# Two more blocks of deformable gathers move from the convolution stage into the attention stage

## The chip, the core and the metric

The kernel runs on one core of a Trainium2 chip. The time is that of one execution on the device, in microseconds (us). A core has TensorE for matrix products (PE in the profile; PEld is its weight load), VectorE (DVE), ScalarE (ACT), GpSimd (POOL) and SyncE (SP), which here only issues transfers. Each engine works off its own list of instructions in order and waits on semaphores for the others. Transfers between the device's memory and the core's memory run on 16 DMA engines; a gather by index is issued by POOL, plain transfers mostly by SP.

## The reference

Four layers on an input of 2 images, 256 channels, 64 x 64 pixels, all in float32:

```python
x = attention_block(x)        # group norm, qkv, 4 heads over 4096 pixels, projection, + normalized x
x = x + position_term         # a linear map of 4 coordinates
x = bottleneck(x)             # 1x1 conv to 64, deformable 3x3 with a mask, 1x1 conv to 256, + x
h = relu(group_norm(x))       # last layer: two deformable 3x3 convolutions on 256 channels
h = deform_conv(h, ...1)
h = relu(group_norm(h))
x = x + deform_conv(h, ...2)
```

A deformable 3x3 convolution works out two offsets for each pixel and each of the 9 taps, here from a 7x7 depthwise and a 1x1 convolution that are merged into one. At each shifted place it interpolates between four neighbouring pixels and multiplies what it gets by the 3x3 weights:

```python
sampled = v00 * (wy0 * wx0) + v01 * (wy0 * wx1) + v10 * (wy1 * wx0) + v11 * (wy1 * wx1)
out = einsum('bckhw,ock->bohw', sampled, w)
```

## The kernel before, in words

**Two stages.** `attention` runs first and `deform` after it. The bottleneck (`class Bottleneck`) has no stage of its own: its steps are generators that the other two call a bit at a time.

**Attention** goes through 1024 tiles `n`, two in each turn of its loop. Four units of 256 tiles are the two images times the two pairs of heads; 16 tiles are one block of 256 query pixels. For each tile PE makes scores (L580), DVE takes their maximum (L592), ACT the exponential (L598), PE transposes it (L610), DVE and ACT copy it (L627, L629), and PE multiplies it by the values (L639). At the end of a block the shares of its four key ranges are combined: `spread` transposes them (L502), DVE copies them out (L504), SP stores them to `share_d` (L506) and loads them spread over the partitions as `f` (L510), and POOL multiplies and adds in `combine` (L519, L520, L525, and L527 in units 0 and 2). DVE copies the next block's products into the same buffer `o` (L471), which has one copy. A dictionary `own` holds which step belongs to which tile. Where a tile has no step of its own, `small` calls `background` in units 2 and 3, and each turn calls it once more. `background(count)` takes `count` steps of the generators in `back`.

**What runs in the background.** In unit 2 `first_batch` starts: the bottleneck's convolution of image 0 (`conv(0)`, 144 steps of two gathers each, L848 into `bfour`; DVE weighs in L1067, POOL adds in L1077 and L1078; four steps of gathers are ahead) and then `early_image`, which normalizes the result and writes it in pixel order to `img3`. In unit 3 `early_samples` follows. It works out offsets and weights of the first blocks of deform (`EARLY` = 2 blocks of 512 pixels; `offsets` L805, L825, L839 on PE, `corners` on DVE). Then `sample` is called in each turn, once, or twice at three turns in eight: it gathers 128 pixels for one tap (512 KB, L848) into a spare buffer of attention and stores them in order to `samp_d` (L1261, on SP). The spare buffers are `xb`, and from the end of the offsets `v`, `k` and `bx` as well, eight in all.

**Deform** goes through 1152 steps `s`: four layers (two images times two convolutions) of 8 blocks of 36 steps (9 taps times 4 groups of 128 pixels). A step's four neighbours come by a gather from `img3` (L848 into `four`); in the first two blocks they come from `samp_d` by a plain load on SP (L1448; the first eight are issued on POOL). Interpolation has two ways:

- *By axis* (a paired step): ACT scales 512 columns (L1471), DVE adds the other 512 (L1477), then ACT 256 (L1486) and DVE 256 (L1490).
- *By corner* (`w4`, four products): ACT 256 (L1486) and DVE three times 256 (L1496).

PE transposes the sample (L1508), ACT copies four of them (L1517), and PE multiplies by the weights (L1527). Beside the steps run `Side` generators with a rate each: `seconds` is the bottleneck's convolution of image 1 (`conv(1)`, 288 gathers, all of its adding on DVE), `offs` the offsets of later blocks, `images` the normalization of the next image (L1372, L1382, L1388).

**What sets the order.** `run` hands the framework the order of PE, ACT, DVE and POOL as written. SP is not in that list: its order comes from the framework's own planning.

Of the kernel before, what the change touches and what calls it, by code (L numbers as in the profile page):

```python
# [11 lines left out]
F32 = mybir.dt.float32  # L12
BF16 = mybir.dt.bfloat16
I32 = mybir.dt.int32
# [6 lines left out]
P = 128  # L21
B, C, H, W = 2, 256, 64, 64
HW = H * W
NB = HW // 512
CM = 64
K2 = 9
EPS = 1e-5
DWK = 7

EARLY = 2  # L30


GH, GW = H + 1, W + 2
# [31 lines left out]
class Net:  # L65
# [115 lines left out]
    def attention(self, bott):  # L181
# [5 lines left out]
        with ExitStack() as ctx:  # L187
# [489 lines left out]
            while n < last + 4 or back or more or any(own.values()):  # L677
                u, d = divmod(n, per_unit)
                if d == 0 and u < len(units):
                    plan_unit(u)  # L680
                    if u == 0:
                        back.append(prepare(1))
                    if u == 1:
                        back.append(bott.before(0, bt, ps))
                    if u == 2:
                        back.append(first_batch())
                    if u == 3:
                        back.insert(0, bott.before(1, bt, ps))
                        back.append(self.early_samples(bott, bt, held, xp, vp, kp, ps))

                def small(at):
                    steps = own.pop(at, ())
                    for f in steps:
                        f()
                    if not steps and u > 1:
                        background(1)

                if n - 1 in pts:
                    p = pts.pop(n - 1)
                    keep(n - 1, p, "ACT")  # L700
# [24 lines left out]

                for _ in range(1 + (n % 16 in (10, 12, 14))):
                    more = self.sample()
                n += 2


    def corners(self, i, pt, mask, base, idx, w4, pool, w=None):
# [13 lines left out]
            nc.scalar.activation(mk, mk, AF.Exp, scale=-1.0)  # L745

        nc.vector.tensor_scalar(p, p, float(H), -1.0, ALU.min, ALU.max)
        whole = pool.tile([P, 4, K2, 2], I32, name="whole")
        nc.vector.tensor_copy(whole, p)
        yield True  # L750
        f = pool.tile([P, 4, K2, 2], F32, name="floor")
        nc.vector.tensor_copy(f, whole)
        g = pool.tile([P, 4, K2, 2], F32, name="above")
        nc.vector.tensor_tensor(g, f, p, ALU.is_gt)
        yield False
        nc.vector.tensor_tensor(f, f, g, ALU.subtract)
# [13 lines left out]
        if mask:  # L770
# [3 lines left out]
            for s in range(2):  # L774
                nc.vector.tensor_mul(w[:, s, :, :, 1], w[:, s, :, :, 1], mk)
            yield False
        for s in range(4):
            nc.vector.tensor_mul(w4[:, :, :, s], w[:, s % 2, :, :, 0], w[:, s // 2, :, :, 1])
        yield True

# [75 lines left out]
    class Bottleneck:  # L856
# [3 lines left out]

        GROUPS = [(0, 1), (2, 3), (4, 5), (6, 7), (8,)]

        CORNERS = NB + EARLY + 1

        def __init__(self, ctx, net):
            self.net = net
# [31 lines left out]
            self.od = wp.tile([P, 512], F32, name="bod")  # L898
            nc.gpsimd.memset(self.od, 0.0)

        def pools(self, ctx, gathers=5, sums=8):
            self.ahead = gathers - 1
            tc = self.net.tc
            return self.kept | {
                n: ctx.enter_context(tc.tile_pool(name=f"bt_{n}", bufs=bufs))
                for n, bufs in (("g", gathers), ("s", sums), ("t", 6), ("x", 2))
            }
# [306 lines left out]
                        nc.sync.dma_start(dst, t[64 * r : 64 * r + 64])  # L1214
                yield True

    def early_samples(self, bott, pools, held, xp, vp, kp, ps):


        nc, a = self.nc, self.a  # L1220
# [26 lines left out]
        for cb in range(2):  # L1247
            t = pools["x"].tile([P, 2, 512], F32, name="bx").rearrange("p u n -> p (u n)")
            whole.append(t)
            wf.append(t[:, : T * 2 * K2].rearrange("p (t o) -> p t o", o=2 * K2))  # L1250
            self.filters(wf[cb], cb, dw, pw)
            yield True
        free = deque(x.rearrange("p u n -> p (u n)") for x in xbs)
        gathers, stores = deque(), deque()

        def gather():


            if len(stores) > 1 and len(free) < 3 or not gathers and stores:
                dst, four = stores.popleft()  # L1260
                nc.sync.dma_start(dst, four)  # L1261
                free.append(four)
            if gathers:
                dst, idx = gathers.popleft()
                four = free.popleft()
                self.gather(four, self.img3[0], idx)
                stores.append((dst, four))
            return gathers or stores

        self.sample = gather  # L1270
        for i in range(EARLY):
            idx = bott.corner.tile([P, 4, K2], I32, name="bidx")
            w4 = self.early[i] = bott.corner.tile([P, 4, K2, 4], F32, name="bw4")
            steps = self.offsets(
                i, xs,
                lambda s, row: wf[s][:, DWK * row : DWK * row + DWK, :].rearrange(
                    "p t o -> p (t o)"
                ),
                self.vec[:, V_PWB : V_PWB + 1],
                bott.base, idx, w4, pools["work"], wide, ps,  # L1280
                odp=lambda: pools["t"].tile([P, 512], F32, name="bst"), y0=rows(i)[0],
                later=ps.later,
            )
            mine = False
            for done in steps:
# [15 lines left out]
    def deform(self, bott):  # L1301
# [5 lines left out]
        with ExitStack() as ctx:  # L1307
# [90 lines left out]
                        yield  # L1398

            IMAGE = 4 + 6 * NB + 1  # L1400
            corners = {(0, 0, i): (None, w4, None) for i, w4 in self.early.items()}

            def offsets(b, l):
                if b == 0:
# [1 line left out]
                wf = self.wf  # L1406
                for i in range(EARLY if (b, l) == (0, 0) else 0, NB):
                    idx = cp.tile([P, 4, K2], I32, name="didx")
                    w4 = cp.tile([P, 4, K2, 4], F32, name="dw4")
                    w = cp.tile([P, 2, 4, K2, 2], F32, name="dwt")  # L1410
                    corners[b, l, i] = idx, w4, w
                    yield from self.offsets(
# [44 lines left out]

            def paired(s):
                n, i, _, j = parts(s)
                return s < ALL and (i >= EARLY if n == 0 else j % 2 == 1)  # L1460

            def share(s, side, axis):
                n, i, k, j = parts(s)
# [77 lines left out]
            def finish(n, i, ob, s):  # L1541
# [14 lines left out]
                        lambda: nc.vector.bn_stats(stats[b][:, ob, i, :], xs)  # L1556
                    )
                else:
                    res = work.tile([P, 512], F32, name="res")
                    nc.sync.dma_start(res, self.x2d[b][rows, cols])  # L1560

                    def second_layer():
# [18 lines left out]
                            self.steps = None  # L1581

            OFFS = 24
            inner = ExitStack()
            second = bott.conv(1, bott.pools(inner, 8, 7), ps)
            for s in range(AHEAD):
                gather(s)
# [3 lines left out]
            next(begun)  # L1591
            load(0, self.xn_d[0], wp)
            offs = [Side(EARLY * BLOCK - LEAD - 6, OFFS / BLOCK, begun)]
            first(0)


            last = Side(0, 1, bott.last(1, bott.kept, ps))
            seconds = Side(0, 0.9, second, lambda s: 2.5 * min(s, EARLY * BLOCK))
            stats[0] = self.norm_stats()
            images = []  # L1600
            for s in range(ALL + 16):
# [15 lines left out]
                if seconds:  # L1617
                    seconds.follow(s)
                    if not seconds.steps:
                        seconds = None  # L1620
                        stats[1] = bott.stats[1]
                        inner.close()
                        images.append(Side(s, 0.9, image(*layers[1])))
                if s % LAYER == LAYER // 2 and 1 <= n < len(layers) - 1:
                    images.append(
# [111 lines left out]
```

## Time and profile before

| | us |
|---|---|
| median of 3 runs (5121.92 to 5128.18) | 5122.12 |
| the profiled execution | 5119.31 |
| its span | 5117.5 |
| PE busy | 4793.9 |
| DVE busy | 4025.2 |
| ACT busy | 3251.1 |
| POOL busy | 2325.6 |

The mean granted clock of TensorE is 0.972. Attention ends near 2965 us; the first step of deform starts at 2990.6. In the page, slices are 128 us each, and a digit is the busy share in tenths. A group line gives busy time and mean of one in ns, then the idle time just before and what ended most of it. In a timeline, a start, a time, an engine, a line and its tiles.

### The profile page before, as it was taken

What the parts mean: (1) busy time and instruction counts of PE and PEld (TensorE: products, weight loads), DVE (VectorE), ACT (ScalarE), POOL (GpSimd) and SP (SyncE); (2) the same over time, 40 slices, a digit from 0 to 9 for tenths busy, and PEclk for the clock granted to TensorE, in tenths of its full rate; (3) what the DMA queues carried; (4) which work ended last, traced back from release to release, by engine and by line L of the source; (5) the groups of instructions that cost most, each with busy time, mean ns of one, the idle gap of its engine ahead of it and who ended that gap; (6) DMA issues with size and microseconds to landing.
All of it is one profiled execution on the core that took longest, in us unless ns stands there. A gap on an engine that the chain in (4) does not pass through costs nothing. (4 is left out here: it accounts for less than half of the span.)

```text
span 5117.5 us, 100364 instructions
## 1 busy us (share of the span) xinstructions
PE 4793.9 (94%) x38200; PEld 2669.1 (52%) x38200; DVE 4025.2 (79%) x7281; ACT 3251.1 (64%) x5869; POOL 2325.6 (45%) x2256
## 2 busy tenths in 40 slices
PE   8999999999999999999999956678999999999998
PEld 5555565555565555565555523334444444444444
DVE  6878867878768888677767668867788888888888
ACT  5676656666666666666656622247876766666666
POOL 0111111111106777565123257775777666666665
PEclk9999999999999999999999977779999999999999
DMA  5231121111112333332547767679999999999998
GB/s 173 61 97 53 43 69 49 35 47 31 55 53 80 103 98 105 93 86 70 164 147 284 274 223 236 202 237 349 358 339 352 363 376 358 366 396 344 349 352 331
DMA packets 367025, 997.68 MB, mean 195 GB/s; under 512 B 61372, under 2 KB 98810, under 8 KB 366542
## 3 DMA queue, kind: packets, MB, share of 16 engines
q0 software_dynamic: 196560, 690.41, 37.4%
q1 hardware_dynamic: 169438, 300.73, 18.0%
q8 instruction: 300, 4.92, 0.4%
q14 instruction: 183, 1.50, 0.1%
q10 hardware_dynamic: 544, 0.13, 0.0%
HBM read 855.36 MB, written 127.35 MB: 192 GB/s over the span
## 5 line engine op out<-in xcount | busy, mean ns | idle before, releaser
L598 ACT ACTIVATE e<-sc,low 128x1024 f32<-128x1024 f32 x1024 | 1146.2, 1119 | 742.3 <-DVE low L592 738.0
L848 POOL DMA_INDIRECT four<-img,didx x1080 | 1152.6, 1067 | 549.9 <-issue 140.3
L592 DVE TENSOR_REDUCE low<-sc 128x1 f32<-128x1024 f32 x1024 | 1205.0, 1218 | 231.7 <-PE sc L580 227.3
L1527 PE MATMUL out<-st,wc 128*128 128x512 f32 x2304 | 1224.8, 614 | 85.7 <-ACT st L1517 41.5
L580 PE MATMUL sc<-k,qs 64*128 64x512 f32 x2048 | 999.1, 606 | 0.5 <-DVE k L368 0.3
L639 PE MATMUL av<-et,v 128*64 128x256 f32 x8192 | 997.7, 386 | 0.0
L580 PE MATMUL sc<-k,q 64*128 64x512 f32 x2048 | 978.2, 605 | 0.0
L519 POOL TENSOR_TENSOR o<-o,f 128x1024 f32<-128x1024 f32 x63 | 149.5, 2373 | 1765.2 <-DMA f<-share_d 1007.7
L610 PEld LDWEIGHTS tt<-ident,e 64*128 64x128 f32 x16384 | 655.3, 139 | 512.9 <-issue 272.7
L629 ACT COPY et<-tt 128x512 f32<-128x512 f32 x1152 | 658.4, 584 | 171.8 <-PE tt L610 170.8
L610 PE MATMUL tt<-ident,e 64*128 64x64 f32 x16384 | 728.0, 227 | 36.3 <-ACT et L629 17.7
L627 DVE COPY et<-tt 128x512 f32<-128x512 f32 x896 | 612.5, 684 | 161.5 <-PE tt L610 160.9
L1496 DVE SCALAR_TENSOR_TENSOR smp<-four,dw,smp 128x256 f32<-128x256 f32 x1296 | 627.2, 484 | 140.5 <-ACT smp L1486 109.0
L639 PEld LDWEIGHTS av<-et,v 128*64 128x64 f32 x8192 | 554.0, 137 | 300.9 <-issue 48.4
L848 POOL DMA_INDIRECT bfour<-img,bidx x576 | 584.1, 1014 | 183.9 <-issue 94.8
L1508 PEld LDWEIGHTS pt<-ident,smp 128*128 128x128 f32 x2304 | 330.5, 144 | 633.9 <-issue 470.9
L1471 ACT ACTIVATE four<-four,dwt 128x512 f32<-128x512 f32 x648 | 465.0, 718 | 200.1 <-DMA four<-img,didx 196.6
L1477 DVE SCALAR_TENSOR_TENSOR four<-four,dwt 128x512 f32<-128x512 f32 x648 | 484.9, 748 | 112.6 <-ACT four L1471 110.2
L1527 PEld LDWEIGHTS out<-st,wc 128*128 128x128 f32 x2304 | 390.9, 196 | 339.3 <-issue 222.8
L580 PEld LDWEIGHTS sc<-k,qs 64*128 64x128 f32 x2048 | 346.9, 189 | 208.7 <-issue 116.8
L1508 PE MATMUL pt<-ident,smp 128*128 128x128 f32 x2304 | 448.8, 278 | 4.6 <-DVE smp L1496 3.1
L805 PE MATMUL pd<-x,wf 128*126 128x512 f32 x840 | 436.0, 601 | 0.0
(189 smaller groups left out, 4743.1 us busy)
## 6 DMA issues: line engine op xcount, KB each, us to landing
f<-share_d SPq DMA_DIRECT2D x128, 256.0 KB
four<-samp_d SPq DMA_DIRECT2D x64, 512.0 KB
xb<-xn SPq DMA_DIRECT2D x55, 512.0 KB
img<-imgt SPq DMA_DIRECT2D x96, 256.0 KB
four<-img,didx POOLq DMA_INDIRECT x1080
xa<-res SPq DMA_DIRECT2D x32, 512.0 KB
samp_d<-xb SPq DMA_DIRECT2D x32, 512.0 KB
xb<-in_x SPq DMA_DIRECT2D x20, 512.0 KB
```

The source lines that it names most:

```text
L580: nc.tensor.matmul(s[:, j, :], lhsT=q[u, i // 2][int(h != j)][halves[j], at : at + P], rhs=k[u][c][halves[j], h, :], start=True, stop=True,)
L592: nc.vector.tensor_reduce(low, s, AX.X, ALU.max, negate=True)
L598: nc.scalar.activation(e.rearrange("p j n -> p (j n)"), s, AF.Exp, bias=blk.low[:, g, c : c + 1], accum_out=blk.sum[:, g, c : c + 1],)
L610: nc.tensor.transpose(pt[:, m, :], e[half, m // 4, m % 4 * P : m % 4 * P + P], self.ident[half, half],)
L627: nc.vector.tensor_copy(dst, pt)
L629: nc.scalar.copy(dst, pt)
L639: nc.tensor.matmul(now["av"][halves[h], :], lhsT=v[u][c][:, m, halves[h]], rhs=ets[j][:, m, h, :], start=(m == 0), stop=(m == 7),)
L848: self.nc.gpsimd.indirect_dma_start(out=dst, out_offset=None, in_=img, in_offset=bass.IndirectOffsetOnAxis(ap=idx, axis=0),)
L1477: nc.vector.scalar_tensor_tensor(uv, four[:, 2 * C :], share(s, 1, 1), uv, ALU.mult, ALU.add)
L1496: nc.vector.scalar_tensor_tensor(smps[s], four[:, c], weight(s, c), smps[s], ALU.mult, ALU.add)
L1508: nc.tensor.transpose(pts[u][:, c, j * P : (j + 1) * P], smp[:, c * P : c * P + P], self.ident,)
L1527: nc.tensor.matmul(outs[ob], lhsT=wc[k][:, c, ob * P : ob * P + P], rhs=sts[u][:, c, :], start=(k == 0 and c == 0), stop=(k == K2 - 1 and ...
```

## The change

- `EARLY` is 4 instead of 2: two more blocks have their offsets worked out and their 72 gathers done during unit 3 of attention, and deform reads 144 steps from `samp_d` instead of 72.
- The early blocks keep weights by axis instead of four products; in deform all steps of the first layer are paired. `w4` is not made there.
- `small` takes two background steps instead of one where `n % 4 == 0`; `sample` is called twice at five turns in eight instead of three.
- The spare buffers become nine (a `pos` tile more), and stores start while fewer than four are free.
- In deform `seconds` has 1.1 extra calls per step over 144 steps instead of 2.5 over 72, and the first steps' `left` and `right` are done ahead of the loop.
- For memory: `above` shares the buffer of `whole`, `bsmp` has 7 buffers in attention instead of 8, `res` of the last layers comes from a pool that is opened later, and the index buffers are 12 instead of 11.

```diff
-EARLY = 2
+EARLY = 4
...
-                        back.append(self.early_samples(bott, bt, held, xp, vp, kp, ps))
+                        back.append(self.early_samples(bott, bt, held, xp, vp, kp, one, ps))
...
                     if not steps and u > 1:
-                        background(1)
+                        background(1 + (n % 4 == 0))
...
-                for _ in range(1 + (n % 16 in (10, 12, 14))):
+                for _ in range(1 + (n % 16 in (2, 6, 10, 12, 14))):
                     more = self.sample()
...
-        whole = pool.tile([P, 4, K2, 2], I32, name="whole")
+        whole = pool.tile([P, 4, K2, 2], F32, name="whole").bitcast(I32)
...
-        g = pool.tile([P, 4, K2, 2], F32, name="above")
+        g = whole.bitcast(F32)
...
-        for s in range(4):
+        for s in range(4 if w4 is not None else 0):
             nc.vector.tensor_mul(w4[:, :, :, s], w[:, s % 2, :, :, 0], w[:, s // 2, :, :, 1])
...
-        CORNERS = NB + EARLY + 1
+        CORNERS = NB + EARLY
...
-        def pools(self, ctx, gathers=5, sums=8):
+        def pools(self, ctx, gathers=5, sums=7):
...
+        xbs.append(one.tile([P, 2, 512], F32, name="pos"))
         free = deque(x.rearrange("p u n -> p (u n)") for x in xbs)
...
-            if len(stores) > 1 and len(free) < 3 or not gathers and stores:
+            if len(stores) > 1 and len(free) < 4 or not gathers and stores:
...
-            w4 = self.early[i] = bott.corner.tile([P, 4, K2, 4], F32, name="bw4")
+            w = bott.corner.tile([P, 4, K2, 4], F32, name="bw4").rearrange("p a k c -> p (a k c)")
+            w = self.early[i] = w.rearrange("p (s j k t) -> p s j k t", s=2, j=4, t=2)
...
-                bott.base, idx, w4, pools["work"], wide, ps,
+                bott.base, idx, None, pools["work"], wide, ps,
...
-            corners = {(0, 0, i): (None, w4, None) for i, w4 in self.early.items()}
+            corners = {(0, 0, i): (None, None, w) for i, w in self.early.items()}
...
-                    w4 = cp.tile([P, 4, K2, 4], F32, name="dw4")
+                    w4 = cp.tile([P, 4, K2, 4], F32, name="dw4") if b or l else None
...
-                return s < ALL and (i >= EARLY if n == 0 else j % 2 == 1)
+                return s < ALL and (n == 0 or j % 2 == 1)
...
-                    res = work.tile([P, 512], F32, name="res")
+                    res = places["res"].tile([P, 512], F32, name="res")
...
+            for s in range(3):
+                left(s)
+            for s in range(2):
+                right(s)
             first(0)
...
-            seconds = Side(0, 0.9, second, lambda s: 2.5 * min(s, EARLY * BLOCK))
+            seconds = Side(0, 0.9, second, lambda s: 1.1 * min(s, EARLY * BLOCK))
...
                         inner.close()
+                        places["res"] = ctx.enter_context(tc.tile_pool(name="df_r", bufs=2))
```

More of the change, by code (lines that the diff above doesn't have):

```diff
@@ L1215, in early_image, with early_samples @@
                 yield True
-    def early_samples(self, bott, pools, held, xp, vp, kp, ps):
+    def early_samples(self, bott, pools, held, xp, vp, kp, one, ps):
         nc, a = self.nc, self.a
@@ L1279, in early_samples @@
                 self.vec[:, V_PWB : V_PWB + 1],
-                bott.base, idx, w4, pools["work"], wide, ps,
+                bott.base, idx, None, pools["work"], wide, ps,
                 odp=lambda: pools["t"].tile([P, 512], F32, name="bst"), y0=rows(i)[0],
-                later=ps.later,
+                later=ps.later, w=w,
             )
@@ L1583, in deform @@
             OFFS = 24
-            inner = ExitStack()
+            inner, places = ExitStack(), {}
             second = bott.conv(1, bott.pools(inner, 8, 7), ps)
```

## The prediction

> **What bounds the kernel now.** I read the slices of the page first, then busy times by stretch, then groups, waits and timelines of the two stretches that the change touches.
>
> ```profile
> PE   8999999999999999999999956678999999999998
> PEclk9999999999999999999999977779999999999999
> ...
> ```
>
> Attention (slices 0 to 22) and the last 1600 us keep PE at nine tenths; slices 23 to 27 do not, and there the granted clock falls too. Busy times by stretch (PE, PEld, DVE, ACT, POOL, clock, DMA share, GB/s):
>
> ```profile
> 3000.00:3100.00 100.00, 44.70 (x137) 22.15 (x138) 79.74 (x200) 19.26 (x35) 72.05 (x71) 0.67 0.73 248
> 3200.00:3300.00 100.00, 66.92 (x200) 30.49 (x200) 90.64 (x211) 23.45 (x42) 77.40 (x74) 0.77 0.67 213
> ...
> 3600.00:3700.00 100.00, 95.42 (x348) 48.57 (x347) 77.47 (x162) 84.95 (x150) 73.15 (x63) 1.00 0.94 348
> ```
>
> This is the start of deform (call it the dip): step 0 (first L1486) starts at 2990.6 us, step 144 at 3524, so 533 us for 144 steps, against 1.5 to 1.7 us per step after that. What fills it, groups of 3040 to 3320 (busy, mean ns | idle before):
>
> ```profile
> L848 POOL DMA_INDIRECT bfour<-img,bidx x206 | 214.6, 1042 | 62.8 <-issue 34.7 <-DMA bfour<-img,bidx 7.3 <-DVE smp L1496 6.7
> ...
> L1067 DVE TENSOR_TENSOR bfour<-bfour,bw 128x512 f32<-128x512 f32 x103 | 70.7, 686 | 15.4 <-DMA bfour<-img,bidx 14.9
> ```
>
> A gather is 1.04 us plus a constant gap of 0.30, start to start 1.35 us, and in these 280 us POOL has no other gap: POOL bounds the dip, with image 1's second convolution (288 gathers). DVE waits only 15 us for it: it is the next bound, close behind.
>
> In unit 3 of attention the early gathers already cost something. Waits of 2660 to 2960, and one round of SP:
>
> ```profile
> POOL o L519 <- DMA f<-share_d: 137.4, 6, 30.8
> DVE o L471 <- POOL avs L525: 10.4, 4, 4.4
> ```
>
> ```profile
> 2861.95 0.34 SPq L1261 DMA_DIRECT2D samp_d<-bx  x1
> ...
> 2885.30 2.79 SPq L1261 DMA_DIRECT2D samp_d<-xb  x2
> 2888.19 0.65 SPq L506 DMA_DIRECT2D share_d<-shares  x1
> 2891.98 1.11 SPq L510 DMA_DIRECT2D f<-share_d  x2
> ```
>
> The shares were copied out by DVE at 2882.1; their store starts at 2888.2, because SP still stands at samp_d stores, and POOL's next multiplication waits for them:
>
> ```profile
> 2804.50 2.36 POOL L519 TENSOR_TENSOR o<-o,f 128x1024 f32<-128x1024 f32 x1 [19.00 <-DMA f<-share_d]
> 2852.95 2.35 POOL L519 TENSOR_TENSOR o<-o,f 128x1024 f32<-128x1024 f32 x1 [24.68 <-DMA f<-share_d]
> 2896.57 2.36 POOL L519 TENSOR_TENSOR o<-o,f 128x1024 f32<-128x1024 f32 x1 [19.73 <-DMA f<-share_d]
> ```
>
> Two rounds here are 92.1 us (2804.50 to 2896.57); in unit 1, with no early gathers, two rounds are 86.3 (1178.0 to 1264.4, same line). And in unit 2 POOL is nearly full:
>
> ```profile
> 1717.76 0.96 POOL L848 DMA_INDIRECT bfour<-img,bidx  x1 [0.27 <-POOL bsmp L1078]
> 1719.03 0.95 POOL L848 DMA_INDIRECT bfour<-img,bidx  x1 [0.30 <-issue]
> 1720.37 0.72 POOL L1077 TENSOR_TENSOR bfour<-bfour 128x256 f32<-128x256 f32 x1 [0.40 <-DVE bfour L1067]
> 1721.17 0.45 POOL L1078 TENSOR_TENSOR bsmp<-bfour 128x128 f32<-128x128 f32 x1
> ```
>
> One step of the convolution there (two gathers, two additions) takes POOL about 4.15 us.
>
> **The change, part by part.** The sum is made against the profiled execution, 5119.3 us (span 5117.5); the median of the runs is 2.8 us higher.
>
> *Two more blocks leave the dip (gain 80).* Now steps 0 to 143 read samp_d through SP, and the convolution is spread over them at 0.9 + 1.1 = 2 calls per step (it was 0.9 + 2.5 over 72 steps, then 0.9); its 300 or so calls end near step 160 instead of 139. By step 144 POOL issues 288 + 8 = 296 gathers: 296 x 1.347 = 399 us from 2999, so 3398 at the earliest. DVE, from start to start of neighbouring instructions: a step by axes 0.67 (L1477) + 0.40 (L1490), both from 3760 to 3970; convolution 0.69 + 0.49 + 0.22; its tail (L1123, L1130, L1129) 1.79 x 16/144 = 0.20; together 2.66 x 144 = 383, and some 10 for index arithmetic: 393 us from about 3005. With the 5.5% that it idles in 3040 to 3320 (15.5 of 280), 416: step 144 near 3422 instead of 3524, 102 less. The stall where image 1 starts to be normalized (steps 132 to 143 take 31 us, their neighbours 20) only moves behind step 144 (12 back), and the convolution's last 17 calls do too (5), and some start-up stays: I take 80. Bounds: POOL without any gap, 3398, gives 109; DVE at the 82% of the whole dip gives 479 us, so 54, less the 17: from 37 to 109. Weights by axis in the 72 early steps are in this sum: three L1496 (1.45 us) become 1.07, and ACT gets one L1471 more (0.72 us), 52 us on an engine that is busy 189 of 534 us there; without that cover they would be paid in full. Dropping dw4 saves four L778 (0.22 us each) for four blocks, under 4 us of DVE, taken as nothing while POOL and DVE are both full; 109 holds it.
>
> *Two more blocks of offsets move into attention (cost 29).* There PE is full. The two blocks of now took 11.0 and 12.3 us of PE in L805 (28 matmuls each); a whole block has 28 x 0.43 = 12, plus 1.9 of L825 and 0.5 of L839: 14.5 each. The round with the two blocks of now was 66.0 us (2603.90 to 2669.91) instead of 43, 23 for two cropped blocks. In the dip the same matmuls lay beside POOL, so nothing comes back there. 25 to 34.
>
> *144 pairs of gather and store, 13 per round instead of 11 (cost 35).* Each pair is 1 MB; in the timeline stores follow at 2.49 us (11 stores, 2861.95 to 2887.78 at the end, DMA share 1.02 in between). A round is: combination to first store 9.0 us, the stores, then 8.4 until f lands. With 13, the short rounds go from 43.6 to 48.6. The long ones (48.4) already wait for another thing, SP at the reload of res until 39.7 us after the combination; the stores would end at 39.8: 48.9. Two rounds: 97.5, against 86.6 free. From the first early gather at about tile 820 (counted below), 144 pairs are 11 rounds; the first two carry the offsets and hide it; 9.2 x 5.4 = 50. Now it is 5.6 x 2.6 = 15. Queued behind POOL's L519 are all later gathers, behind SP's stores the shares, q halves and xb loads; DVE's L471 waits for o, and L592 and the copies of the next tile stand behind it. Bounds: if the store of the shares slips in front, 15 are won; if the long rounds grow by 5 too, 55.
>
> *Denser calls in units 2 and 3 (cost 20 and 11).* Counting the free places: 15 and 18 calls in even and odd blocks of 16 tiles become 17 and 23, so 8.25 steps (two calls each) per block become 10. POOL then needs 20 x 4.15 + 4.4 + 6.8 (combinations, with L527 in one) = 94.2 us per two blocks. PE, by the starts of L592, needs 80.7 (unit 0 has 40.3 per block) plus 20 x 0.45 (two blocks of now take 89.65 with 16.5 steps, 1.6 of them idle): 89.6. POOL becomes the bound by 4.6 per pair; 144 steps are 7.2 pairs: 33, less the 14 of idle PE now: 20, from 0 (four gathers ahead absorb it) to 45 (twice the wait). Two calls in one place also use the one PSUM bank twice with no attention between them, so PE waits for a copy (0.6 to 0.7 us and its queue): some eight in the image, a dozen in the offsets, about 0.55 each: 11; 0 to 30. In return the convolution ends some 50 tiles earlier and the early blocks start at tile 812 or so, not 888; at 13 per 16 tiles the last store is issued near tile 1005 of 1024.
>
> *One pool buffer less (bsmp 7), the aliased tiles, the res pool, the preamble of left and right:* nothing; four bsmp are filled per transposition and at most three more before it, and the others have no instruction on the path. If bsmp waits once per transposition for a PE slot (2.7 us), 40 transpositions cost 0 to 30 of POOL, inside the 45.
>
> Sum: -80 + 29 + 35 + 20 + 11 = +15: 5119.3 + 15 = 5134, as a median 5137.
>
> [...] In 1600 to 2080 L1067 takes 898 ns on DVE in the mean (median 683, longest 2430), against 686 in the dip, where POOL adds nothing: 0.21 us each, and the count of 144 stays, so the sum has nothing for it. [...]
>
> **Rivals.** (1) Faster: the store of the shares does not fall behind the stores. SP's order is not written out in the kernel (only PE, ACT, DVE and POOL are), so it may come elsewhere; then rounds are 43 us, and instead of +35 there are -15: 5087. For it speaks that the store waited 1.0 us only in the first such round, against it 5.6 and 5.8 in the next short ones. It decides below 10 us of cost. (2) No difference: POOL's four steps of lead absorb the denser calls and PE does not meet the bank, -31: 5106; with the dip's gain nearer 60, 5126. Against it, POOL's runs without a gap in unit 2. (3) Slower still: the early blocks start 50 tiles later than I count; 14 pairs are left after the last tile, 2.5 us each, with nothing beside them (+35), 5172; about the same comes from DVE at 82% in the dip (+43).
>
> **How the numbers follow.** A measurement tells about 0.2%, 10 us, from no change. My sum 0.43, rival 1 0.30, rival 2 0.12, rival 3 0.15. My own case runs from 5112 to 5165 by its bounds taken half; a sixth of it lies within 0.2%. Faster: rival 1 and a third of rival 2, 0.34; same: the rest of 2 and 0.08 of mine, 0.16; slower 0.50. The range goes from rival 1 with a dip of 85 to rival 3 with 10 on top: 5080 to 5185.
>
> **What would show it.** Right: in the dip, POOL's gathers back to back to about 3400 on the old clock of the deform start, step 144 some 430 us after step 0; in unit 3, rounds of L519 near 48.6 with L471 waiting for POOL's avs in nearly all; in unit 2, two rounds near 94 with DVE's L1067 waiting for gathers; first early gather near tile 820. Wrong: short rounds still at 43, conv rounds at 90, or early gathers still running after the last L592.

## The result and the profile after

The changed kernel takes 5197.15 us in the median of 4 runs (5192.82 to 5199.73); the kernel before, beside it on the same chip, takes 5122.82 (4 runs). The ratio is 1.0141, with an interval of 1.0127 to 1.0154: 74 us slower. The profiled execution has a span of 5193.6 us, 76.1 more than before. In the new file the lines of attention keep their numbers, those of deform are higher by two (L1486 is now L1488, L1490 L1492, L1527 L1529), and the store of a sample is L1262.

The page's slices of the kernel after (130 us each) show how the picture has turned. The weak place of before, counted from slice 0 (5, 6, 6, 7 and 8 tenths in slices 23 to 27) has become a little shallower and a slice shorter (6, 7, 7, 7 in slices 24 to 27), and three slices of attention, 18, 21 and 23, have fallen to eight tenths:

```profile
PE   8999999999999999998998986777999999999998
...
PEclk9999999999999999999998997888999999999999
```

In the dip, the stretches of the kernel after (PE, PEld, DVE, ACT, POOL, clock, DMA share, GB/s), counted from a first step at 3149.0:

```profile
3160.00:3260.00 100.00, 61.97 (x198) 28.95 (x198) 83.41 (x203) 50.57 (x86) 74.72 (x69) 0.81 0.90 307
3360.00:3460.00 100.00, 76.52 (x252) 35.96 (x250) 91.26 (x191) 54.71 (x95) 79.00 (x69) 0.88 0.87 293
```

PE issues 198 to 252 matmuls in 100 us there, against 137 to 200 before. Step 144 comes 426.1 us after step 0 (before 533.4). So the part of the change in deform worked; the loss is in attention. The lengths of its stretches, from the first L592 of a unit and the first steps of deform:

| us | before | after | difference |
|---|---|---|---|
| unit 2 | 740.1 | 803.7 | +63.6 |
| unit 3 until step 0 | 800.0 | 896.0 | +96.0 |
| steps 0 to 143 | 533.4 | 426.1 | -107.3 |
| steps 144 to 287 | 233.8 | 258.1 | +24.3 |
| steps 288 to the end | 1359.7 | 1360.4 | +0.7 |

The rest of the 76.1 us, 1.2 less, lies ahead of unit 2.

To see what the 160 us in attention are made of, PE's time is split into work and idling, since PE is the engine that attention waits for. First the stretches of units 2 and 3 before, then the same after (the columns are those above):

```profile
1450.50:2190.60 740.10, 728.74 (x7906) 438.12 (x7904) 581.22 (x831) 492.39 (x919) 446.14 (x489) 1.00 0.31 90
2190.60:2990.60 800.00, 769.00 (x7895) 455.98 (x7891) 565.85 (x907) 510.56 (x950) 268.93 (x286) 0.98 0.51 172
```

```profile
1449.30:2253.00 803.70, 756.00 (x7978) 447.35 (x7976) 602.70 (x861) 499.09 (x931) 521.79 (x585) 0.97 0.32 92
...
2253.00:3149.00 896.00, 806.82 (x7923) 467.09 (x7919) 552.81 (x893) 509.67 (x946) 259.75 (x263) 0.95 0.65 231
```

Unit 2 is 27.3 us of busy PE longer and 36.3 us of idle PE (740.10 - 728.74 = 11.4 idle before, 47.7 after); unit 3 is 37.8 busy and 58.2 idle longer. In both, the granted clock has fallen by 0.03 (from 1.00 to 0.97, and from 0.98 to 0.95). PE's groups say which instructions it is. Unit 2 before and after (busy, mean ns, then idle time before them and who ended it):

```profile
L639 PE MATMUL av<-et,v 128*64 128x256 f32 x2048 | 249.7, 386 | 0.0
...
L1088 PE MATMUL pm<-ident,bsmp 128*128 128x128 f32 (+1 forms) x112 | 18.4, 286 | 1.5 <-POOL bsmp L1078 0.7 <-DVE res L550 0.3 <-DVE shares L504 0.3
```

```profile
L639 PE MATMUL av<-et,v 128*64 128x256 f32 x2048 | 257.5, 395 | 0.0
...
L1088 PE MATMUL pm<-ident,bsmp 128*128 128x128 f32 (+1 forms) x140 | 26.2, 295 | 30.5 <-POOL bsmp L1078 29.3 <-DVE shares L504 1.0
```

Unit 3 before and after:

```profile
L639 PE MATMUL av<-et,v 128*64 128x256 f32 x2096 | 257.9, 389 | 0.0
...
L610 PE MATMUL tt<-ident,e 64*128 64x64 f32 x4128 | 190.4, 228 | 15.5 <-DVE et L627 10.4 <-ACT et L629 4.1
L805 PE MATMUL pm<-v,bx 128*126 128x512 f32 (+3 forms) x56 | 23.3, 573 | 0.0
```

```profile
L639 PE MATMUL av<-et,v 128*64 128x256 f32 x2096 | 272.8, 405 | 0.0
...
L610 PE MATMUL tt<-ident,e 64*128 64x64 f32 x4128 | 194.8, 231 | 63.6 <-DVE et L627 42.0 <-ACT et L629 21.1
L805 PE MATMUL pm<-v,bx 128*126 128x512 f32 (+3 forms) x112 | 47.8, 585 | 0.0
```

Three things are to be read from these lines. In unit 2 PE's transposition of the convolution's samples (L1088) waits 29 us for POOL's sums, where it waited 1 us before. In unit 3 PE's transposition of attention's own tiles (L610) waits 48 us longer than before, for copies of DVE and ACT that are late. And in both units the same products by the values (L639, the same count) have become slower, by 7.8 and 14.9 us. Added up over the two units, L639, L580, L610 and L544, whose counts are the same, take 31 us more busy time than before. The last section shows that this is the clock.

What is late in unit 3 is the combination of shares, as the waits of the kernel after in 2640 to 3060 show:

```profile
POOL o L519 <- DMA f<-share_d: 199.2, 8, 27.0
...
DVE o L471 <- POOL avs L525: 65.6, 9, 12.2
```

L471 on DVE now stalls in each round, 7.3 us in the mean; it did so four times for 10.4 us in all. Behind it on DVE stand L592 and L627 of the next tiles, behind them PE. One round of SP, after the combination of 2694.47:

```profile
2703.50 2.36 SPq L1262 DMA_DIRECT2D samp_d<-xb  x2
...
2724.33 5.49 SPq L1262 DMA_DIRECT2D samp_d<-xb  x3
2732.08 0.32 SPq L1262 DMA_DIRECT2D samp_d<-pos  x1
2734.67 0.32 SPq L1262 DMA_DIRECT2D samp_d<-v  x1
2735.08 0.38 SPq L506 DMA_DIRECT2D share_d<-shares  x1
2739.03 1.11 SPq L510 DMA_DIRECT2D f<-share_d  x2
```

DVE had copied the shares out 10.9 us before their store was issued: SP stood at the last of 13 stores of samples, each of which waits for its gather. In the nine rounds from 2591.2 on, the store of the shares is issued 4.6 to 14.4 us after that copy; in the five full rounds of the kernel before it was 1.1 to 7.9. The rounds that follow from it, by POOL's multiplications:

```profile
2639.65 2.36 POOL L519 TENSOR_TENSOR o<-o,f 128x1024 f32<-128x1024 f32 x1 [21.86 <-DVE low L592]
2694.47 2.34 POOL L519 TENSOR_TENSOR o<-o,f 128x1024 f32<-128x1024 f32 x1 [26.61 <-DMA f<-share_d]
2743.79 2.34 POOL L519 TENSOR_TENSOR o<-o,f 128x1024 f32<-128x1024 f32 x1 [22.58 <-DMA f<-share_d]
```

These are 54.8 and 49.3 us. Over nine rounds (2591.2 to 3053.2) the mean is 51.3; before, in the same part, rounds were 43.0 to 48.4.

### The profile page after: what moved, and what is told of

It is laid out like the page before. It is cut to its first block, busy times and chain, and to the rows that moved or that the text cites. A ratio compares the mean times of both kernels' runs of the same rounds, so it can differ in the third digit from the quotient of the medians.

```text
span 5193.6 us, 100673 instructions
## 1 busy us (share of the span) xinstructions
PE 4815.3 (93%) x38200; PEld 2666.5 (51%) x38200; DVE 3995.5 (77%) x7177; ACT 3300.6 (64%) x5941; POOL 2334.2 (45%) x2256
## 3 DMA queue, kind: packets, MB, share of 16 engines
q0 software_dynamic: 196560, 690.41, 36.6%
q1 hardware_dynamic: 190750, 378.07, 21.9%
## 5 line engine op out<-in xcount | busy, mean ns | idle before, releaser
L592 DVE TENSOR_REDUCE low<-sc 128x1 f32<-128x1024 f32 x1024 | 1205.4, 1218 | 280.0 <-PE sc L580 276.5
L1529 PE MATMUL out<-st,wc 128*128 128x512 f32 x2304 | 1228.9, 616 | 83.7 <-ACT st L1519 50.6
L848 POOL DMA_INDIRECT four<-img,didx x1008 | 1068.3, 1060 | 527.2 <-ACT smp L1488 132.8
L639 PE MATMUL av<-et,v 128*64 128x256 f32 x8192 | 1020.3, 392 | 0.0
L580 PE MATMUL sc<-k,qs 64*128 64x512 f32 x2048 | 998.5, 607 | 1.2 <-ACT e L598 0.9
L580 PE MATMUL sc<-k,q 64*128 64x512 f32 x2048 | 984.0, 606 | 0.0
L610 PEld LDWEIGHTS tt<-ident,e 64*128 64x128 f32 x16384 | 652.1, 139 | 577.1 <-issue 281.8
L610 PE MATMUL tt<-ident,e 64*128 64x64 f32 x16384 | 728.0, 227 | 87.8 <-DVE et L627 47.4
L627 DVE COPY et<-tt 128x512 f32<-128x512 f32 x896 | 612.8, 684 | 147.9 <-PE tt L610 147.4
L639 PEld LDWEIGHTS av<-et,v 128*64 128x64 f32 x8192 | 562.2, 139 | 316.7 <-issue 69.6
L848 POOL DMA_INDIRECT bfour<-img,bidx x576 | 611.3, 1061 | 182.1 <-issue 87.7
L1529 PEld LDWEIGHTS out<-st,wc 128*128 128x128 f32 x2304 | 388.4, 196 | 322.0 <-issue 205.8
L1473 ACT ACTIVATE four<-four,dwt 128x512 f32<-128x512 f32 x576 | 413.4, 718 | 135.0 <-DMA four<-img,didx 131.8
L1479 DVE SCALAR_TENSOR_TENSOR four<-four,dwt 128x512 f32<-128x512 f32 x576 | 431.2, 749 | 73.9 <-ACT four L1473 71.1
L580 PEld LDWEIGHTS sc<-k,qs 64*128 64x128 f32 x2048 | 346.6, 189 | 237.4 <-issue 147.8
L805 PE MATMUL pd<-x,wf 128*126 128x512 f32 (+2 forms) x784 | 397.4, 589 | 0.0
```

What stands on the lines that cost most here:

```text
L580: nc.tensor.matmul(s[:, j, :], lhsT=q[u, i // 2][int(h != j)][halves[j], at : at + P], rhs=k[u][c][halves[j], h, :], start=True, stop=True,)
L592: nc.vector.tensor_reduce(low, s, AX.X, ALU.max, negate=True)
L610: nc.tensor.transpose(pt[:, m, :], e[half, m // 4, m % 4 * P : m % 4 * P + P], self.ident[half, half],)
L627: nc.vector.tensor_copy(dst, pt)
L639: nc.tensor.matmul(now["av"][halves[h], :], lhsT=v[u][c][:, m, halves[h]], rhs=ets[j][:, m, h, :], start=(m == 0), stop=(m == 7),)
L805: nc.tensor.matmul(pd[:m, r0 * W : r1 * W], lhsT=wt(s, t), rhs=src[:, (y + r0 - y0) * W : (y + r1 - y0) * W], start=(n == 0), stop=(n == l ...
```

## The experiments

They landed on three chips, and on two of them the kernel before is slower, so that each ratio is against the kernel before on the same chip: 5289 us beside e1 to e4, 5310 beside c_before, c_after, e5 and e6, and 5124 beside e7, e8, e9 and v1. On the chip of 5310 the change itself was run once more, and it cost less.

> The kernel before again, for its trace beside the others on one chip. Every theory: its usual time.

> The changed kernel again, for its trace and time beside the others on one chip. Every theory: 1.2 to 1.6% slower than the kernel before.

On the chip of 5310 us the kernel after took 5326.6 us, a ratio of 1.0029 (1.0015 to 1.0043). Unit 2 is 65.0 us longer (755.0 to 820.0) and unit 3 85.9 (847.3 to 933.2), about as much as on the first chip; but the dip gives back 162.4 us (605.1 to 442.7) instead of 107. Rounds before are 49.0 to 54.9 us there already, and after 50.0 to 58.2. So the expectation of 1.2 to 1.6% was missed: what the change is worth depends on the chip.

One thing sets the two slower chips apart in every run. ACT waits there for something that the trace calls "remote", which is its word for a wait whose end it can put down to no instruction and no transfer. Ahead of ACT's copies in unit 3 of the kernel before, then of the kernel after, on the chip of 5310:

```profile
ACT et L629 <- remote: 27.8, 5, 8.4
```

```profile
ACT et L629 <- remote: 42.0, 5, 10.1
```

In the six profiled executions on a chip of 5123 or 5124, those of the result among them, ACT has no such wait. Where they fall in c_after, PE, ACT and DVE stand still together, and the shares are late before SP has anything to do with them: DVE has copied them out 43.7 to 46.8 us after the combination (29.7 to 34.7 on the first chip), and their store is issued within 1.1 us of that. So the rounds are long there for another reason than on the first chip. In the first 144 steps of deform such waits of ACT come to 150.7 us in c_before and 38.5 in c_after, which goes with the larger gain there. What they are isn't known.

**The shares on another queue (e1, e2).** The store and loads of the shares are taken off SP and issued by ACT, one and two turns of the loop later; e1 does so in the kernel after, e2 in the kernel before.

```diff
-                    nc.sync.dma_start(d, t)
+                    sends.append(store)
+                    sends.append(load)
...
+                if sends:
+                    sends.popleft()()
```

> The changed kernel with the store and the two loads of the shares issued on ScalarE's queue, one turn after the transposition, instead of SP's. If the shares' place behind samp_d stores on SP sets the rounds of unit 3, rounds between L519 fall from 48 to 54 us to 43 to 46, the waits of L471 for POOL's avs (65.6 us) fall below 10, and the time falls by 50 to 75 us, to 5120 to 5147. If the 26 transfers of 512 KB per round as such set them, rounds stay above 48 and the time above 5180. Unit 2 stays at about 804 us in either case.

> The same edit in the kernel before. By the first theory the 15 us that the rounds of unit 3 cost there go: 5100 to 5115. By the second nothing changes: 5115 to 5125.

e1: 1.0057 (1.0041 to 1.0074), e2: 1.0001 (0.9988 to 1.0014). The store's wait on SP is gone in e1, yet rounds remain at 50 to 56. The waits of e1 in 2740 to 3160 (line numbers are 7 higher in this file) show why it doesn't decide:

```profile
POOL o L526 <- DMA f<-share_d: 159.6, 6, 29.3
...
ACT et L636 <- remote: 42.8, 9, 7.2
```

ACT stands nine times, 4.8 us in the mean, at the waits that the trace calls "remote". They are not the edit's doing, since the kernel before and the kernel after have them on the other slower chip. And the shares of e1 are late ahead of their store, copied out 41.2 to 43.3 us after the combination in these rounds. In c_after, on the other slower chip, they hardly wait for SP to begin with; if that holds here too, taking them off SP could win little. The expectation of e1 was missed, e2 found no difference, and neither decides anything for the first chip.

**Thirteen pairs in a round, alone (e4).**

```diff
-                for _ in range(1 + (n % 16 in (10, 12, 14))):
+                for _ in range(1 + (n % 16 in (2, 6, 10, 12, 14))):
```

> The kernel before with two more gathers and stores per block of 16 tiles alone (13 instead of 11). By the queue of SP, its 5 rounds of unit 3 get 5 us longer each and there is one fewer: 5130 to 5150. If SP's order hides two more pairs, 5115 to 5127.

0.9982 (0.9972 to 0.9991): it costs nothing on that chip. Rounds are 48.8 to 53.9, no longer than the kernel before's 49 to 55 on a chip like it, and the gathers end 16 tiles sooner. The expectation was missed; where rounds with 11 pairs are as long already, the run says nothing on a chip where they are 43.

**The stores on another queue (e5, e9).** Instead of the shares, the stores of samples are moved, from SP to POOL, which issued their gathers; e5 in the kernel after, e9 in the kernel before.

```diff
-                nc.sync.dma_start(dst, four)
+                nc.gpsimd.dma_start(dst, four)
```

> The changed kernel with the stores to samp_d on POOL's queue (as written, six calls behind their gather), so that SP has no wait for gathers ahead of the shares and no engine gets a new wait for a transfer that is still under way. If the place of the shares on SP sets the rounds of unit 3, they fall from 48 to 54 us to 43 to 46 and the time by 45 to 75 us. If the transfers as such set them, rounds stay within 2 us and so does the time within 15.

> The kernel before with its stores to samp_d on POOL's queue alone. By the place of the shares on SP its five full rounds go to 43 to 46 us: 10 to 35 us faster. If the transfers set the rounds: within 10 us.

e5 takes 5237.2 us, against 5326.6 of the kernel after on the same chip: 89 us less (45 to 75 were expected), 0.9876 (0.9847 to 0.9904) of the kernel before. The nine rounds with 13 pairs go from 50.0 to 58.2 down to 44.6 to 47.5. The same view of POOL in e5:

```profile
2649.12 2.35 POOL L519 TENSOR_TENSOR o<-o,f 128x1024 f32<-128x1024 f32 x1 [9.85 <-DMA f<-share_d]
2694.51 2.36 POOL L519 TENSOR_TENSOR o<-o,f 128x1024 f32<-128x1024 f32 x1 [6.76 <-DMA f<-share_d]
2740.73 2.36 POOL L519 TENSOR_TENSOR o<-o,f 128x1024 f32<-128x1024 f32 x1 [10.35 <-DVE low L592]
```

And unit 3 of the kernel after on that chip, then of e5:

```profile
2269.30:3202.50 933.20, 837.15 (x7923) 477.83 (x7919) 552.49 (x893) 511.49 (x947) 260.26 (x263) 0.93 0.63 222
```

```profile
2264.60:3110.60 846.00, 792.77 (x7923) 460.06 (x7919) 551.99 (x893) 511.61 (x947) 346.65 (x407) 0.98 0.69 245
```

The same gathers, the same bytes and the same number of matmuls (7923): unit 3 is 87.2 us shorter. Half of that is idle PE (96.1 to 53.2), the other half busy PE (837.2 to 792.8), as the clock rises from 0.93 to 0.98. So it is the place of the stores, on SP or on POOL, and not the number of transfers or bytes, that makes the rounds long. With the issuing engine their DMA queue changes as well, as far as the pages tell (in that of the kernel after, SP's transfers are on a `hardware_dynamic` queue, 378.07 MB, and those of POOL on a `software_dynamic` one, 690.41 MB), which no run separates. By which wait the stores on SP do it on this chip isn't shown either: the store of the shares had not waited on SP in c_after, and what e5 no longer has in unit 3 is the wait on "remote" (42.0 us in c_after, none in e5).

For a chip like the first, e8 and v1 below, which ran on the chip of 5124, are the comparison. e8 has the stores on SP, 13 pairs in a round, shares that wait 6.0 to 14.7 us for their store in the nine rounds, and rounds of 48.5 to 54.8. v1 has the stores on POOL, 16 pairs in a round, shares whose store is issued within 0.1 us of their copy in its seven full rounds, and rounds of 45.3 to 51.0. There the wait of the shares on SP and the long rounds go together.

In the kernel before, e9's edit is worth 10 us, the least that was expected: 0.9983 (0.9973 to 0.9992), with rounds of 42.5 to 46.7 instead of 43.0 to 48.4, as far fewer rounds are held up there.

No more than 0.3 to 0.4 us of issue was moved per store (a single one takes 0.32 in the rounds of the kernel after shown here), but with it the semaphore wait ahead of each store, and the time fell by 89 us in e5.

**The denser calls, alone (e3).** In the kernel before:

```diff
-                        background(1)
+                        background(1 + (n % 4 == 0))
```

> The kernel before with the denser background calls alone. If it is POOL's lack of time in unit 2 that costs, unit 2 gets 50 to 65 us longer (804 against 740), PE's L1088 waits for POOL's bsmp 25 us or more in 1550 to 2050, and the time is 5160 to 5185, since the work that leaves unit 3 gives back about 13. If instead the seven bsmp buffers of the changed kernel are the cause, unit 2 stays within 15 us of 740.

1.0117 (1.0100 to 1.0134), some 62 us, with nothing in return. Unit 2 of e3 and PE's first wait in it:

```profile
1449.80:2264.20 814.40, 761.19 (x7978) 450.01 (x7976) 605.57 (x860) 501.39 (x930) 522.80 (x585) 0.97 0.30 91
```

```profile
PE pm L1088 <- POOL bsmp L1078: 27.6, 13, 3.8
```

The kernel before with this one edit has unit 2 of the kernel after: as long (814 to 820 on such chips), with the same clock and the same wait of L1088. On the same chip e4, which leaves unit 2 as it was, takes 751.8 us for it, 62.6 less, and L1088 waits 0.7 us there. e3 keeps all eight `bsmp` buffers, so the one that the change takes away has no part in it.

**What in the denser calls costs it (e6, e7, e8).** e6 lets DVE do POOL's two additions. e7 makes POOL's first addition small and leaves out the rest of that sum. e8 keeps the number of calls, but spreads them over the turns: two in the first of a turn's two places and one in the second, in every turn, where the change has two in both places of every other turn. (The two places are the calls `small(n)` and `small(n + 1)`.)

```diff
-                engine = (nc.gpsimd, nc.vector)[b]
+                engine = nc.vector
```

```diff
-                engine.tensor_add(four[:, :, 0:2, :], four[:, :, 0:2, :], four[:, :, 2:4, :])
+                    engine.tensor_add(
+                        four[:, :, 0:2, :8], four[:, :, 0:2, :8], four[:, :, 2:4, :8]
+                    )
```

```diff
-                        background(1 + (n % 4 == 0))
+                        background(1 + (at == n))
```

> The changed kernel with the two additions per step of image 0's convolution on DVE, as image 1 has them: POOL gives up about 1.4 of its 4.15 us per step, DVE gets about 0.7. If POOL without free time makes unit 2 longer, by making PE wait for its sums, unit 2 shrinks by 30 to 60 us and so does the time. If two calls in one place (the PSUM bank, DVE) do it, unit 2 stays or grows with DVE's 0.7 us per step, 0 to 40 us.

> The changed kernel with the first of the two additions per step of image 0's convolution cut to 8 of 64 columns on POOL (the rest of that sum is left out), so that a step takes POOL about 0.5 us less of 4.15 and DVE nothing more. If POOL without free time makes unit 2 longer, unit 2 loses 30 to 55 of the 65 us that the denser calls cost it. If the denser calls cost by their place (two in one small, PE and DVE), it loses under 15.

> The changed kernel with the same number of background calls in two blocks (40), but two at every tile n and one at n + 1 instead of two and two in every other turn. If two calls one behind the other in both places of one turn cost (the bursts), unit 2 loses 20 to 50 us. If POOL's total sets it, it stays within 10.

e6 took 5392.7 us, 66 more than the kernel after on its chip, with a unit 2 of 870 instead of 820. Both expectations were missed. L1088's wait for the sums is gone, but others took its place. Its waits in 1550 to 2050 show DVE as the bound, with POOL's gathers waiting for it:

```profile
POOL bfour L848 <- DVE bsmp L1078: 184.7, 52, 8.8
```

So DVE has no more room for the denser convolution than POOL (in part it is the chip: ACT's "remote" waits in unit 2 are 29.3 us here and 8.0 in c_after). e8 took 5195.4 us in its one run, with a unit 2 of 806.0, within 2.3 of the kernel after: that both places of a turn are doubled one behind the other is not what costs. It still puts two calls into one place, in every turn, so that it says nothing on those. e7 took 5170.1 us in its one run; its unit 2:

```profile
1449.60:2228.20 778.60, 747.23 (x7978) 444.58 (x7976) 597.91 (x860) 498.81 (x930) 455.28 (x585) 0.99 0.32 95
```

25.1 us came back, less than the 30 expected: 16.3 of idle PE (the wait of L1088 went from 29.3 to 12.9) and 8.8 of busy PE, with the clock at 0.99 instead of 0.97. POOL's additions are thus a cause. With most of POOL's extra work away (446.1 busy before, 521.8 after, 455.3 here) two fifths of the 63.6 us return. Of the 38.5 that remain, 12.2 are the same wait of L1088, shorter but still there, and some 15 are work that has only moved: 28 more L1088, 40 more L1098 and 4 more L1120 lie in unit 2 than before, and unit 3 has 11.8 us less of these lines after the change.

**A version from these (v1).** The kernel after, with the stores on POOL, denser calls in unit 3 alone, and two samples in each turn to make up for the later start:

```diff
-                        background(1 + (n % 4 == 0))
+                        background(1 + (u > 2 and n % 4 == 0))
...
-                for _ in range(1 + (n % 16 in (2, 6, 10, 12, 14))):
+                for _ in range(2):
...
-                nc.sync.dma_start(dst, four)
+                nc.gpsimd.dma_start(dst, four)
```

> A version meant to beat both: the changed kernel with the stores to samp_d on POOL's queue, two samples in every turn, and the denser calls in unit 3 alone. If the place of the shares on SP and the denser calls in unit 2 are what the change pays, unit 2 takes what it takes in the kernel before, rounds of unit 3 stay below 48 with 16 pairs each, and the time is 100 to 150 us below the kernel before on that chip. If 16 pairs fill the DMA engines, rounds go above 50 and it gains under 60.

5088.9 us: 0.9929 (0.9913 to 0.9946) of the kernel before, and below the 5114.6 of e9 on the same chip, which has two early blocks. That is 35 us less than before, where 100 to 150 were expected. The profiled execution took 5104.9, the longest of the four. Unit 2 of v1 is that of before again:

```profile
1450.00:2187.70 737.70, 726.52 (x7906) 436.15 (x7904) 580.75 (x831) 492.67 (x919) 445.21 (x489) 1.00 0.30 90
```

Unit 3 takes 868.1 us (68 more than before, 28 less than after) with 16 pairs in rounds of 45.3 to 51.0, four of the seven at or above the 48 that were expected as the most, and steps 0 to 143 take 427.0. The early gathers start at tile 874 and end at 1019 of 1024. So four early blocks are worth having once they don't stand in front of the shares and unit 2 keeps the calls that it had.

## Why the prediction was right and wrong

The sign was right: my sum was +15 us on the profiled execution, and +76.1 was measured. The time itself, 5197, lies above the range, which ended at 5185. Term by term:

*The dip, -80.* Right. Step 144 was to come some 430 us after step 0, and came after 426.1. The stretch up to step 288, where the moved convolution and the stall end up, gives 107.3 - 24.3 = 83.0 back. DVE was to be what limits it: it is at 83 to 91% in the two stretches shown, and POOL is at 75 to 79 with gathers. Behind step 144, 24.3 us were given back where I counted 17; the 144 steps themselves gained a little more than I had.

*Offsets, +29.* Right: PE's L805, L825 and L839 take 24.5 + 3.9 + 2.1 = 30.5 us more in unit 3.

*The counted places.* Right: I put the first early gather near tile 820 and the last store near 1005; the first was issued at tile 828, the last gather at 1004, the last store at 1005. Rival 3, early blocks that start 50 tiles late, didn't happen.

*Pairs, +35.* The mechanism was right, its size too small. The short rounds were to be 48.6 us and are 48.0 to 49.3. What failed is the step for the long rounds: "already wait for another thing, SP at the reload of res until 39.7 us after the combination; the stores would end at 39.8: 48.9". I took the later of two waits, but they stand one behind the other. In SP's list the last store is followed by the store of the block's result (`xa`, L557), the reload of `res` waits for that store to land, and the shares' store comes behind the reload. The kernel before in its round of 2804.50, then the kernel after in its round of 2639.65:

```profile
2838.96 0.32 SPq L1261 DMA_DIRECT2D samp_d<-bx  x1
2839.37 0.39 SPq L557 DMA_DIRECT2D xa<-res  x1
2844.18 0.37 SPq L214 DMA_DIRECT2D res<-xa  x1
2844.64 0.42 SPq L506 DMA_DIRECT2D share_d<-shares  x1
```

```profile
2680.06 0.32 SPq L1262 DMA_DIRECT2D samp_d<-xb  x1
2680.47 0.42 SPq L557 DMA_DIRECT2D xa<-res  x1
2685.28 0.37 SPq L214 DMA_DIRECT2D res<-xa  x1
2685.74 0.42 SPq L506 DMA_DIRECT2D share_d<-shares  x1
```

The last store of these rounds is issued 39.6 to 40.4 us after the combination, as written, but the reload moved behind it, from 39.7 to 44.5 to 45.6, and the rounds are 53.0 to 54.8. The shares are ready when they were before and wait 12.4 to 14.4 us on SP there. Nine rounds come to 462 us, 72 more than nine free ones of 43.3, where I had 50 in all; with the 15 that before has, +57 instead of +35, which is about the bound that I had named ("if the long rounds grow by 5 too, 55"). PE's own account has +48 for it, as idle time ahead of L610. Rival 1, in which the shares slip past the stores, didn't happen by itself; v1, with the stores on POOL, shows that its place was the right one to look at.

*Denser calls, +20 and +11.* The direction was right: "POOL becomes the bound". The expected sign of it, DVE's L1067 waiting for gathers, did not come (0.2 us in that stretch). It is PE that waits for POOL's sums at L1088: 29.3 us in 13 waits, near the 33 that I had worked out. Two blocks of unit 2 were to take 94 us and take about 100. The step that failed is "less the 14 of idle PE now", a matter of a few us. PE's idle time of before has not gone away: ahead of L610 there were 8.9 us, and there are 12.3. Idle PE is 36.3 us more in unit 2, against 31 for both terms, of which a part was meant for unit 3. The second term, two calls in one place meeting the one PSUM bank, was tested by no run, since e8 keeps two calls in one place. Rival 2, in which four steps of lead absorb the calls, is refuted by e3.

*The term that was missing: the clock.* This is the largest step that failed. The sum held only waits and work, at durations of before, and put the effect of new waits on the speed of TensorE at nothing without a reason, though the prediction had seen the clock fall in the dip. PE's own instructions became slower as well: 31.3 us over L639 (+22.7), L580 (+5.5), L544 (+1.8) and L610 (+1.3), and 4.5 on the convolution's three, whose counts over both units are the same. The last section shows how this hangs on the waits. In e5, e7 and unit 2 of v1 it came back with the idle time.

Against my +15 this makes: 1.5 on the offsets, 13 on the rounds, 5 on unit 2's idle time, 36 on the clock, 9 of other idle time in unit 3 (waits below 6 us each, not tested by a run), less 3 in the dip: 61.5, against the 61.1 that are missing.

*The weighing, L1067.* Right: the sum had nothing for it, and in 1600 to 2080 L1067 takes 856 ns in the mean after the change, against 898 before. In e6, where POOL makes none of the convolution's additions, it takes 715 in the same window, so that most of what it takes beyond the 686 of the dip goes with those additions; by what it does isn't shown.

## What to carry to other kernels

A transfer that many wait for should not stand in a queue behind transfers that themselves wait for something, and two waits in one queue add up where one stands behind the other (here the shares stood 12.4 to 14.4 us on SP in the long rounds); moving 144 stores to the engine that had issued their gathers brought 89 us on one chip, by a wait that isn't shown there. Filling an engine's last free places can make the engine that sets the time wait for it: in unit 2 POOL's work went from 446.1 to 521.8 us, and the wait of L1088 for its sums from 0.7 to 29.3; count what it has left. And where TensorE is the bound, as in attention here, price idle time on it above its length, for the reason that follows: 36.3 us of it in unit 2 came with some 11 of slower matmuls, 58.2 in unit 3 with some 21, and e5 got back 42.8 with 44.4. A change should also be measured on more than one chip, where the kernel can run on more than one: this one cost 1.4% on the first and 0.3% on another.

## What the runs showed of the hardware

I had not expected how much a short gap on TensorE costs. The kernel after around one of L1088's waits, of 2.90 us, that ends at 1980.98:

```profile
1970.00:1978.00 8.00, 8.00 (x99) 4.99 (x97) 7.33 (x10) 5.50 (x11) 6.66 (x9) 1.00 0.60 197
1978.00:1986.00 8.00, 5.09 (x22) 2.38 (x21) 1.68 (x3) 2.99 (x6) 6.57 (x9) 0.65 0.24 68
1986.00:1994.00 8.00, 8.00 (x83) 4.42 (x82) 5.97 (x9) 4.09 (x8) 6.53 (x8) 0.93 0.30 89
```

Sixteen L639 in a row before the wait, and the next sixteen just after it:

```profile
1972.75 1.95 PE L639 MATMUL av<-et,v 128*64 128x256 f32 x16
1981.39 3.68 PE L639 MATMUL av<-et,v 128*64 128x256 f32 x16
```

Sixteen matmuls of one kind take 1.95 us and then 3.68. In narrower windows the granted clock is 1.00 up to 1980.3, 0.50 from 1980.4 to 1987.2, and 1.00 again from 1987.3. PE is busy for 6.21 us of that half-speed stretch, of which half, 3.1, is lost, beside the 2.90 of the wait: some 6 us in all, an estimate.

The units as a whole agree. In units 2 and 3 of both kernels the trace has the granted clock at 1.0 or 0.5 and nothing between, and at 0.5 for 3.41 us or a multiple of it at a time: 22 such stretches begin there after the change, 6 before. In the kernel after, 242 of the L639 lie within them and take 641 ns in the mean; 3872 lie at full clock and take 384, as the 4092 at full clock in the kernel before do. So the slower products are the clock and nothing else. Each of the 22 stretches follows 3.41 us in which PE sat idle for 1.8 to 3.4.

Over whole units the two move together: idle PE and clock are 11.4 us and 1.00 in unit 2 before, 31.4 and 0.99 in e7, 47.7 and 0.97 after; in unit 3, e5 got as much from faster matmuls (44.4 us) as from less idling (42.8).

Two things stay open: what the waits are that the trace calls "remote" on the two slower chips, and with them why the same kernel before takes 5123 us on one chip and 5289 or 5310 on others, with 72 us of that in the first 144 steps of deform; and why the waits in unit 3 went when the stores moved to POOL in e5.
